# A linear-attention and sparse-FFN kernel: the q products come first in each step, q copies are issued one slot earlier, sums and loads are reordered

## The chip, the cores and the metric

The kernel runs on one core of one Trainium2 chip. A core has a matrix engine (TensorE, PE in the profile, its weight loads PEld), a vector engine (VectorE, DVE), a scalar engine (ScalarE, ACT), GpSimd (POOL) and SyncE (SP), which here issues nearly all DMAs. Each engine works through its own list of instructions in order. The metric is device time in microseconds; lower is better.

## The reference

The input x has two batches of 1024 rows of 512. The reference computes, with a layernorm before and after each of two blocks and a residual around each:

```python
x = x + _layernorm(_L0_attn_ref(_layernorm(x, axis=-1), Wq, Wk, Wv, Wo), axis=-1)
x = x + _layernorm(_L0_ffn_ref(_layernorm(x, axis=-1), w_gate, w_up, w_down), axis=-1)
```

The attention is linear and causal: 16 query heads, 4 key and value heads, head size 128. q and k are rotated (rope), then passed through elu(.) + 1; a scan keeps a running sum of k v^T and of k, and each output is q times the state, divided by q times the sum of k. The feed-forward block is `silu(x Wg) * (x Wu)`, of which the two largest of every four neighbours (by absolute value) are kept, times `w_down`; the hidden width is 2048.

## The kernel before

**Strassen-like products.** Every large product is cut into 2 x 2 blocks and done with seven block products instead of eight (`strassen`, L114). Its generator yields after each of the seven, so that the caller can put other work between: the products come in the order 1, 2, 6, 5, 7, 4, 3. Products 1, 6, 7 and 4 add up in one PSUM bank ("cb"), product 2 has "ca", products 5 and 3 add up in "ce". After 1, 6 and 7 ScalarE copies the bank's partial sum (`keep`, L125), and DVE adds it to another bank (L134, L144, L150). The weight combinations that the products need are sums of weight quarters (`sums`, L419). For the first pass over q, k, v they are made on the chip from loaded quarters; for everything later POOL prepares them in the background (`prepare`, L453) and SP stores them to DRAM and loads them again.

**Steps.** The attention goes through 16 steps: two passes (each has half of the heads) over eight chunks of 128 rows of both batches. For step n + 1, `kv_products` (L652) and `q_products` (L675) make k, v and four blocks of q. `features` (L622) does the rope and elu of a block: two DVE multiplies (L629, L635), a POOL add (L641), two ScalarE functions (L643, L644), a DVE combine (L645). A q block is then turned in 32 x 32 squares by DVE (L549), stored to DRAM (`q_store`), loaded in another order (`q_load`, four DMA issues, L562) and copied by ScalarE into place (`q_copy`, L712), which finishes the transpose.

Each step has four slots, one for each group (batch, key head). `scores(n, i)` (L715) multiplies the transposed k with the copied q and DVE masks the result; `attend(n, i)` (L731) multiplies by v and by the state; DVE takes the reciprocal of the denominator and ScalarE scales four heads (L754). The output block goes the same way over DRAM (`o_store`, `o_load`, `o_copy`), and the output projection of step n - 1, `o_products` (L809), runs in step n. In the second pass its end is a layernorm and residual: POOL adds the first pass's part (L843), DVE normalizes, POOL adds x (L846), and SP stores the rows for the feed-forward part.

**Order.** PE, POOL and SP keep the order in which the program text emits instructions (`manual_schedule`, L877). On DVE and ACT a planner orders by its own estimate, except for the very first part on DVE. In a step, the calls `first(i)` and `second(i)` (L908, L929) hold the slot's copies, stores, loads, attend and scores; the products of the next step and of the previous output lie between them. Before the change the order of a step is: kv products of n + 1 in slot 0, q products in slots 0 to 2, output products in slots 2 and 3. The four sums of `o_copy(n, 3)` (L799 to L803) are emitted together; one of them (L802) runs on POOL. `q_copy(n, i + 1)` is issued in `first(i)`, right before `attend(n, i)` and `scores(n, i + 1)` of the same slot.

**Ends.** At the start x, the weight quarters, the rope table, the next x blocks and the output weights are loaded on two queues (L434 to L444). At the end of the attention the first feed-forward rows are normalized and transposed (`ffn_input`, L193), and the first two gate products are run early (L1022 on). The feed-forward part goes over four groups of 512 rows: gate and up products, the choice of two of four, the down product, and `ffn_output` (L354), which normalizes and adds the residual for four row tiles.

Of the kernel before, what the change touches and what calls it, by code (L numbers as in the profile page):

```python
# [35 lines left out]
def kernel(  # L36
# [21 lines left out]

    ident = const.tile([P, P], F32, name="ident")
# [13 lines left out]
    eps = const.tile([P, 1], F32, name="eps")  # L73
    nc.gpsimd.memset(eps, LN_EPS)
# [24 lines left out]
    def layernorm_scale(src, tag):  # L99

        st = small.tile([P, nc.vector.BN_STATS_DIM], F32, tag=f"st{tag}", name="st")
        nc.vector.bn_stats(st, src)
        mv = small.tile([P, nc.vector.BN_AGGR_DIM], F32, tag=f"mv{tag}", name="mv")
        nc.vector.bn_aggr(mv, st)
        sd = small.tile([P, 1], F32, tag=f"sd{tag}", name="sd")
        nc.scalar.activation(sd, mv[:, 1:2], AF.Sqrt, bias=eps)
        rs = small.tile([P, 1], F32, tag=f"rs{tag}", name="rs")
        nc.vector.reciprocal(rs, sd)
        return mv[:, 0:1], rs
# [4 lines left out]
    def strassen(pools, shape, product, c11, c12, c22, done):  # L114
# [24 lines left out]
        e = bank("ce")  # L139
# [4 lines left out]
        nc.vector.tensor_tensor(c22, s3, e, ALU.add)  # L144
# [5 lines left out]
        nc.vector.tensor_tensor(c12, s2, e, ALU.add)  # L150
# [170 lines left out]
    def down(hf):  # L321


        def product(bank, i, start):
# [3 lines left out]
            for jb in range(NJB):  # L328
                for j in range(2):
                    for k in range(2):  # L330
                        nc.tensor.matmul(
                            bank[:, j, :],
                            hf[jb][hi][:, k, j * P : (j + 1) * P],
                            w[:, jb, k, :],
                            start=(start and jb == 0 and j == 0 and k == 0),
                            stop=(jb == NJB - 1 and j == 1 and k == 1),
                            skip_group_check=True,
                        )
# [10 lines left out]
                lambda t: nc.scalar.copy(y[:, 0:2, 256:512], t),  # L349
            )  # L350
# [3 lines left out]
    def ffn_output(m, tt, xt_, y):  # L354
        b, c = place(m, tt)
        mean, rs = layernorm_scale(y, "y")
        yn = pool["ln"].tile([P, DM], F32, tag="ln", name="fyn")
        normalize(yn, y, mean, rs)
        nc.gpsimd.tensor_tensor(yn, xt_, yn, ALU.add)  # L359
# [59 lines left out]
    def sums(t, engine):  # L419
        a11, a12, a22, s2, s4, s3, s1 = (t[:, i] for i in range(7))  # L420
        for o, i0, i1, op in (
            (s1, s3, a22, ALU.add),
            (s3, a11, s3, ALU.subtract),
            (s2, s1, a11, ALU.subtract),
# [9 lines left out]
    xt = {0: load_x(0)}  # L434
# [3 lines left out]
    load_quarters(wq_sb, q_quarter, (nc.scalar, nc.sync))  # L438
    rope_sb = rawp.tile([P, NC, 3, HD // 2], F32, name="rope_sb", bufs=1)
    nc.scalar.dma_start(out=rope_sb, in_=rope.rearrange("(c p) t d -> p c t d", p=P))  # L440
    xt[1] = load_x(1)
    wo_sb = new_factors("wo", 4, 256)
    load_quarters(wo_sb, o_quarter, (nc.sync,))
    xt[2] = load_x(2)  # L444
# [177 lines left out]
    def features(src, c, dst):  # L622

        half = HD // 2
        cos = rope_sb[:, c, 0, :].unsqueeze(1).broadcast_to([P, 8, half])
        sin = rope_sb[:, c, 1:3, :].unsqueeze(1).broadcast_to([P, 4, 2, half])
# [25 lines left out]
    def kv_products(n):  # L652
        c = n % NC
# [13 lines left out]
        features(raw, c, f)  # L667
# [7 lines left out]
    def q_products(n):  # L675
        c = n % NC
        raw = [rawp.tile([P, REP, HD], F32, tag="raw", name="qraw", bufs=4) for _ in range(3)]

        def feature(i, src):
            f = qp.tile([P, REP, HD], F32, tag="qf", name="qf", bufs=1)  # L680
            features(src, c, f)
# [28 lines left out]
    def q_copy(n, i):  # L710
        t = qp.tile([P, REP, P], F32, tag="qT", name="qT")
# [64 lines left out]
    later = []  # L776
# [13 lines left out]
    def o_copy(n, i, t=None):  # L790
# [6 lines left out]
        else:  # L797
            t1, t2, t3, t4 = (factor(n, 3 + k, 1) for k in range(4))
            nc.vector.tensor_tensor(by_block(t1), t, by_block(of[n, 0]), ALU.subtract)  # L799
            nc.vector.tensor_tensor(t2, of[n, 2], t1, ALU.subtract)  # L800
            t3_engine = nc.gpsimd if n + 1 < STEPS else nc.vector
# [47 lines left out]
    def load_pass(place, name, blocks, width, of_):  # L849
        t = new_factors(name, blocks, width)  # L850
        for f in range(7):
            nc.sync.dma_start(out=t[:, f], in_=of_[:, f])
# [258 lines left out]
```

## Time and profile before

The times are of whole runs; the profile is one of these executions.

| what | value |
|---|---|
| median of 5 runs | 1494.82 us (1491.52 to 1501.59) |
| the profiled execution, its time | 1501.59 us |
| its span (first to last instruction) | 1499.9 us |
| mean granted TensorE clock | 0.955 |
| PE busy | 1335.4 us, 89% |
| DVE busy | 866.8 us, 58% |
| ACT busy | 518.6 us, 35% |
| POOL busy | 324.6 us, 22% |
| first score of step 0, 1, 8, 15 | 60.9, 95.7, 469.8, 822.4 us |
| first gate product, end of the early gates and last output product | 876.3, 917.9 us |

A line of the profile's lists gives an engine, a line of the kernel (L12) and what it made from what, then the idle time of the engine before it and what ended that wait. In the list of waits the numbers are microseconds in total, how often, and the longest. In the timeline they are the start, the duration, and in brackets the idle time before. The table by stage has for each stretch its length, the busy time of each engine with its instructions, the granted clock, the DMA share and GB/s.

### The profile page before, as it was taken

The page shows a single profiled execution, that of the slowest core. Times are in us where ns is not written, and L with a number is a line of the kernel's source. Part 1 is how long each engine was busy: PE and PEld are TensorE (multiplying, and loading weights), DVE is VectorE, ACT ScalarE, POOL GpSimd, SP SyncE. Part 2 cuts the span into 40 slices and gives each one's busy share as a digit, 9 for nine tenths or more (in the row PEclk, how much of TensorE's full clock was granted, in tenths as well). Part 3 has the DMA queues.
Part 4 walks back from the last instruction along what each step waited for, and adds up shares of the span by engine and source line. Part 5 has one row for each costly group of instructions (what it writes and reads, how often), then busy time and mean ns, then how long its engine had stood idle before and what let it go on. Part 6 is the DMA issues. An engine that isn't in the chain of part 4 may idle for free. (4 is left out here: it accounts for less than half of the span.)

```text
span 1499.9 us, 17626 instructions
## 1 busy us (share of the span) xinstructions
PE 1335.4 (89%) x5888; PEld 1047.6 (70%) x5888; DVE 866.8 (58%) x1550; ACT 518.6 (35%) x1053; POOL 324.6 (22%) x259
## 2 busy tenths in 40 slices
PE   4779888897888879899889599999999999999997
PEld 2446566565566547666666488888888888888886
DVE  5657656745645546675666523982667166725662
ACT  2444444433333334444434332321332133213311
POOL 0323223222323414434442111011001100110001
PEclk9979989999998889999999799999999999999999
DMA  6344566565876657765655635545654465445412
GB/s 227 108 161 142 183 200 203 176 196 172 269 238 175 183 203 245 246 215 180 226 186 174 218 99 195 157 124 175 197 150 124 175 198 151 123 176 173 116 57 84
DMA packets 199019, 262.56 MB, mean 175 GB/s; under 512 B 18192, under 2 KB 124688, under 8 KB 194832
## 3 DMA queue, kind: packets, MB, share of 16 engines
q1 hardware_dynamic: 196800, 259.07, 54.3%
q10 hardware_dynamic: 2128, 2.36, 0.5%
q8 instruction: 47, 0.77, 0.2%
q14 instruction: 44, 0.36, 0.1%
HBM read 177.73 MB, written 83.62 MB: 174 GB/s over the span
## 5 line engine op out<-in xcount | busy, mean ns | idle before, releaser
L125 ACT COPY u<-cb 128x512 f32<-128x512 f32 (+1 forms) x252 | 126.4, 501 | 468.3 <-PE cb L225 178.6
L641 POOL TENSOR_TENSOR u<-u,r 128x512 f32<-128x512 f32 x80 | 106.3, 1330 | 359.8 <-DVE r L635 183.3
L817 PE MATMUL cb<-wo,of 128*128 128x256 f32 x512 | 142.9, 429 | 36.6 <-ACT u L125 31.7
L817 PEld LDWEIGHTS cb<-wo,of 128*128 128x128 f32 x512 | 108.3, 217 | 73.4 <-issue 45.1
L718 PE MATMUL sc<-qT,kT 128*128 128x512 f32 x128 | 78.1, 696 | 71.6 <-ACT qT L712 71.6
L608 PE MATMUL cb<-wq,xf 128*128 128x512 f32 x256 | 124.0, 607 | 1.7 <-ACT u L125 1.7
L225 PE MATMUL cb<-fxt,wgu 128*128 128x256 f32 x512 | 117.9, 381 | 1.4 <-ACT u L125 1.4
L225 PE MATMUL cb<-fxnT,wgu 128*128 128x256 f32 x512 | 116.9, 379 | 0.0
L645 DVE SCALAR_TENSOR_TENSOR qf<-u,r 128x512 f32<-128x512 f32 x64 | 67.0, 1047 | 81.0 <-ACT r L644 69.3
L754 ACT ACTIVATE o<-nm,den 128x128 f32<-128x128 f32 x256 | 75.7, 365 | 108.6 <-DVE den L751 102.9
L225 PEld LDWEIGHTS cb<-fxt,wgu 128*128 128x128 f32 x512 | 96.6, 190 | 17.0 <-ACT u L125 4.2
L745 PE MATMUL nm<-v,am 128*128 128x129 f32 x512 | 100.6, 288 | 7.7 <-ACT state L767 5.0
L225 PEld LDWEIGHTS cb<-fxnT,wgu 128*128 128x128 f32 x512 | 97.0, 190 | 13.2 <-ACT u L125 0.2
L643 ACT ACTIVATE r<-u 128x512 f32<-128x512 f32 x80 | 50.5, 631 | 133.2 <-POOL u L641 132.6
L173 POOL TENSOR_TENSOR h<-h 128x512 f32<-128x512 f32 x16 | 23.9, 1496 | 332.3 <-DVE ht L170 332.3
L608 PEld LDWEIGHTS cb<-wq,xf 128*128 128x128 f32 x256 | 49.2, 195 | 61.1 <-issue 49.4
L744 PE MATMUL nm<-state,qT 128*128 128x129 f32 x448 | 90.1, 284 | 1.1 <-DVE state L769 1.1
L745 PEld LDWEIGHTS nm<-v,am 128*128 128x128 f32 x512 | 81.7, 205 | 10.2 <-ACT state L767 5.4
L144 DVE TENSOR_TENSOR y<-u,ce 128x256 f32<-128x256 f32 (+1 forms) x20 | 9.5, 474 | 126.2 <-ACT u L125 126.2
L744 PEld LDWEIGHTS nm<-state,qT 128*128 128x128 f32 x448 | 75.1, 201 | 9.9 <-issue 6.2
L718 PEld LDWEIGHTS sc<-qT,kT 128*128 128x128 f32 x128 | 21.2, 209 | 77.3 <-ACT qT L712 77.3
L608 PE MATMUL cb<-wkv,xf 128*128 128x256 f32 x256 | 71.0, 402 | 4.3 <-ACT u L125 2.9
(150 smaller groups left out, 2577.2 us busy)
## 6 DMA issues: line engine op xcount, KB each, us to landing
wgu<-gs SPq DMA_DIRECT2D x112, 256.0 KB, 2.8
wgu<-us SPq DMA_DIRECT2D x112, 256.0 KB, 2.7
wd<-d_dram SPq DMA_DIRECT2D x28, 1024.0 KB, 4.8
qb<-blocks SPq DMA_DIRECT2D x64, 256.0 KB, 2.1
landed<-qb SPq DMA_DIRECT2D x256, 64.0 KB, 2.2
ob<-blocks SPq DMA_DIRECT2D x60, 256.0 KB, 2.3
landed<-ob SPq DMA_DIRECT2D x240, 64.0 KB, 2.2
xf<-xf SPq DMA_DIRECT2D x16, 896.0 KB, 4.7
```

The lines of the kernel that those rows point to most:

```text
L125: nc.scalar.copy(t, b)
L173: (engine or nc.gpsimd).tensor_tensor(b12, b22, b12, ALU.subtract)
L225: nc.tensor.matmul(bank[:, j, :], w[:, k, j, :], xf[xi][:, k, :], start=(start and j == 0 and k == 0), stop=(j == 1 and k == 1), skip_grou ...
L608: nc.tensor.matmul(bank.rearrange("p h d -> p (h d)"), x_[:, xi, k, :], w[:, wi, k, :], start=(start and k == 0), stop=(k == 1), skip_grou ...
L641: nc.gpsimd.tensor_tensor(u, u, r, ALU.add)
L643: nc.scalar.activation(r, u, AF.Relu, scale=-1.0)
L645: nc.vector.scalar_tensor_tensor(dst, u, 0.0, r, ALU.max, ALU.add)
L718: nc.tensor.matmul(sc.rearrange("p h t -> p (h t)"), kT[n][:, 2 * b + j, :], qT[n, i].rearrange("p h t -> p (h t)"), start=True, stop=True,)
L744: nc.tensor.matmul(dst, q[:, h, :], state[b, j], start=True, stop=False)
L745: nc.tensor.matmul(dst, a[:, h, :], v, start=(c == 0), stop=True)
L754: nc.scalar.activation(t[:, h, :], nmv[:, h // 2, h % 2, 0:HD], AF.Copy, scale=den[:, h // 2, h % 2 : h % 2 + 1],)
L817: nc.tensor.matmul(bank.rearrange("p h d -> p (h d)"), of[n, xi][:, k, :], w[:, wi, k, :], start=(start and k == 0), stop=(k == 3), skip_g ...
```

## The change

In each step the q products of step n + 1 now come first (slots 0 and 1), then the kv products (slots 1 and 2), then the output products of step n - 1 (slots 2 and 3). `q_copy` is issued one slot earlier, with three buffers in place of two, and the stores and loads before it move to match. Three of the four output sums move into `o_sums`, which is called after the kv features. The residual add and the store behind it move into later slots. In each half slot the output's store, the q load and the output's load come in this order. The weight loads of the second pass come in the order in which the products use them, a few per slot. The rope table is loaded a chunk at a time.

At the start, x is loaded in two halves on two queues, the weight sums run on POOL instead of DVE, later x blocks and output weights are loaded behind the first step's input, the square root's table is loaded by a small activation ahead of its first use, and the q products of step 1 run in full ahead of step 0, its kv products inside step 0. At the attention's end the feed-forward transposes begin one step earlier, in another PSUM pool, and the first gate runs between the slots. The ring of feed-forward weights has 15 buffers, not 16. In the last down product, products 5 and 3 finish one row tile before the other; the last two row tiles take their statistics in two halves and add the residual on DVE.

```diff
     def layernorm_scale(src, tag, st=None):
+        if st is None:
+            st = layernorm_stats(src, tag)[:, 0:1, :]
+        else:
+            nc.vector.bn_stats(st[:, 1, :], src)
...
-        e = bank("ce")
+        rows = range(shape[1]) if split else [slice(0, shape[1])]
+        es = [bank("ce")[:, r] for r in rows]
+        e = es if split else es[0]
...
-        nc.vector.tensor_tensor(c12, s2, e, ALU.add)
+        for r, er in zip(rows, es):
+            nc.vector.tensor_tensor(c12[:, r], s2[:, r], er, ALU.add)
...
+            split = isinstance(bank, list)
+            blocks = [(jb, j) for jb in range(NJB) for j in range(2)]
+            if split:
+                blocks.sort(key=lambda block: block[1])
...
-        nc.gpsimd.tensor_tensor(yn, xt_, yn, ALU.add)
+        (nc.vector if last else nc.gpsimd).tensor_tensor(yn, xt_, yn, ALU.add)
...
-    xt = {0: load_x(0)}
+    def load_rope(n):
+        t = rawp.tile([P, 3, HD // 2], F32, tag="rope", name="rope")
+        c = n % NC
+        nc.sync.dma_start(out=t, in_=rope[c * P : (c + 1) * P])
+        rope_sb[n] = t
+
+    xt, rope_sb = {}, {}
+    xt[0] = xp.tile([P, B, DM], F32, tag="x", name="x")
+    for b, engine in enumerate((nc.sync, nc.scalar)):
+        engine.dma_start(out=xt[0][:, b, :], in_=x[b, 0:P, :])
...
-    load_quarters(wq_sb, q_quarter, (nc.scalar, nc.sync))
-    rope_sb = rawp.tile([P, NC, 3, HD // 2], F32, name="rope_sb", bufs=1)
-    nc.scalar.dma_start(out=rope_sb, in_=rope.rearrange("(c p) t d -> p c t d", p=P))
-    xt[1] = load_x(1)
+    load_quarters(wq_sb, q_quarter, (nc.sync, nc.scalar))
+    load_rope(0)
+    root = const.tile([P, 1], F32, name="root")
+    nc.scalar.activation(root, eps, AF.Sqrt)
...
-        t = qp.tile([P, REP, P], F32, tag="qT", name="qT")
+        t = qp.tile([P, REP, P], F32, tag="qT", name="qT", bufs=3)
...
+    def o_sums(n):
+        t2, t3, t4 = (factor(n, 4 + k, 1) for k in range(3))
+        nc.vector.tensor_tensor(t2, of[n, 2], of[n, 3], ALU.subtract)
+        t3_engine = nc.gpsimd if n + 1 < STEPS else nc.vector
+        t3_engine.tensor_tensor(t3, t2, of[n, 0], ALU.subtract)
+        nc.vector.tensor_tensor(t4, of[n, 1], t2, ALU.subtract)
...
+        for i in (1, 2, 6, 5, 7, 4, 3):
+            f = FACTORS[i][0]
+            nc.sync.dma_start(out=t[:, f], in_=of_[:, f])
+            yield
...
-            finish(sums(wkv_sb, nc.vector))
+            finish(sums(wkv_sb, nc.gpsimd))
             step_input(0, xns)
-            finish(sums(wq_sb, nc.vector))
+        xt[1] = load_x(1)
+        load_rope(1)
+        load_quarters(wo_sb, o_quarter, (nc.sync,))
+        xt[2] = load_x(2)
+        wq_sums = sums(wq_sb, nc.gpsimd)
+        run(wq_sums, 2)
         finish(kv_products(0))
+        finish(wq_sums)
...
             def first(i):
...
-                if i < 3:
-                    q_copy(n, i + 1)
+                if i < 2:
+                    q_copy(n, i + 2)
                 elif more:
-                    q_copy(n + 1, 0)
+                    q_copy(n + 1, i - 2)
...
+                if i < 2 and n > 0:
+                    o_copy(n - 1, i + 2)
+                elif i > 1 and more:
+                    o_copy(n, i - 2)
                 if i == 2 and more:
                     q_store(n + 1, 3)
+                if i > 0 and more:
                     o_store(n, i - 1)
                 elif i == 0 and n > 0:
                     o_store(n - 1, 3)
+                if i == 0:
+                    q_load(n, 3)
+                elif more:
+                    q_load(n + 1, i - 1)
+                if i > 0 and more:
+                    o_load(n, i - 1)
+                elif i == 0 and n > 0:
+                    o_load(n - 1, 3)
+                if i == 2 and n + 2 < STEPS:
+                    load_rope(n + 2)
+                next(preparing, None)
+
+            def second(i):
+                for k in ((0,), (1, 2), (), ())[i] if more else ():
+                    q_store(n + 1, k)
                 attend(n, i)
...
             first(0)
+            if n > 0:
+                run(qpr, 2)
...
+            second(0)
+            first(1)
+            finish(qpr)
...
+            kvp = kv_products(n + 1)
+            run(kvp, 3)
...
             second(1)
             first(2)
+            finish(kvp)
...
+            if n > 0:
+                o_sums(n - 1)
...
+            run(opr, 2)
...
             second(2)
             first(3)
...
+            run(opr, 1)
+            k_transposed(n + 1)
+            run(opr, 2)
...
             second(3)
             finish(opr)
```

## The prediction

> **What bounds the kernel now.** First the page's head and its row of slices for TensorE and its clock.
>
> ```profile
> span 1499.9 us, 17626 instructions
> PE 1335.4 (89%) x5888; PEld 1047.6 (70%) x5888; DVE 866.8 (58%) x1550; ACT 518.6 (35%) x1053; POOL 324.6 (22%) x259
> PE   4779888897888879899889599999999999999997
> PEclk9979989999998889999999799999999999999999
> ```
>
> TensorE is the fullest engine, but it has holes in the first 25 of 40 slices and its clock dips there. Next comes the table by stage. I cut it at the first score matmul of steps 1, 8 and 15, and at the first gate product after the attention.
>
> ```profile
> 0.00:95.71 95.71, 57.78 (x193) 34.63 (x193) 62.39 (x118) 37.51 (x80) 24.34 (x26) 0.92 0.45 157
> 95.71:469.81 374.10, 323.36 (x1389) 234.34 (x1389) 218.75 (x405) 150.06 (x340) 107.09 (x85) 0.92 0.61 195
> 469.81:822.41 352.60, 311.78 (x1341) 223.07 (x1341) 212.92 (x390) 148.41 (x335) 126.06 (x100) 0.95 0.64 205
> 822.41:917.86 95.45, 76.83 (x347) 63.00 (x346) 35.38 (x87) 30.70 (x68) 12.75 (x10) 0.87 0.46 146
> 917.86:1499.90 582.04, 565.64 (x2625) 492.52 (x2623) 337.33 (x552) 151.90 (x231) 54.34 (x39) 1.00 0.49 151
> ```
>
> After each stretch's length stand PE, PEld, DVE, ACT and POOL busy, then the granted clock. The last stretch, the feed-forward part, runs TensorE at 97% and full clock: little is to be had there but its tail. The other 918 us are the place. Third, TensorE's waits.
>
> ```profile
> PE sc L718 <- ACT qT L712: 71.6, 25, 8.3
> PE cb L817 <- ACT u L125: 31.7, 13, 4.6
> PE pst L539 <- DVE x L112: 16.9, 2, 8.7
> ```
>
> The scores wait for the q copy (71.6 us), the output products for ScalarE's copy of a partial product (31.7), the first transposes for the first normalize (16.9). Last, a window at one long score wait, with the plainer kind from step 12 below it.
>
> ```profile
> 184.80 1.77 POOL L802 TENSOR_TENSOR of<-of 128x512 f32<-128x512 f32 x1 [8.35 <-DVE of L800]
> 186.53 2.48 POOL L641 TENSOR_TENSOR u<-u,r 128x512 f32<-128x512 f32 x2
> 187.82 0.63 ACT L643 ACTIVATE r<-u 128x512 f32<-128x512 f32 x1 [6.16 <-POOL u L641]
> 190.62 0.60 ACT L712 COPY qT<-landed 128x512 f32<-128x512 f32 x1
> 191.27 2.07 PE L718 MATMUL sc<-qT,kT 128*128 128x512 f32 x2 [8.22 <-ACT qT L712]
> ...
> 726.17 1.14 ACT L754 ACTIVATE o<-nm,den 128x128 f32<-128x128 f32 x4 [2.13 <-DVE den L751]
> 727.19 0.63 ACT L712 COPY qT<-landed 128x512 f32<-128x512 f32 x1
> ```
>
> At 184.80 POOL stood 8.35 us at an output sum; the feature adds came behind it, ScalarE stood at the feature, and the q copy, which needs neither, stood behind that. At 727 the copy merely stands behind the attend's own scalings, and the scores wait 2.23 us after attend has ended.
>
> **The floor of a step.** Step 14 runs from 777.75 to 822.41, 44.66 us, and its rows show waits of 1.66 and 0.19: 42.8 without them. Steps 1 to 7 also transpose two x blocks, 0.43 each (the kf transposes take 709.63 to 710.06): 43.7.
>
> **Steps 1 to 7 (374.1 us, floor 306).** Of 68 us over the floor, waits of the kinds above are 36.8 + 15.7 + 1.5 = 54. That leaves 14 for half clock and small bubbles.
> - Copies a slot ahead, three qT buffers. A q copy now has some 11 us between its issue and its scores instead of following the same attend. The scaling that holds it is 1.14 us, the long chain above about 6; both fit. I take all 36.8.
> - Sums behind the features. POOL's L802 no longer stands ahead of L641, so the 8 us chain goes. The sums' readers (products 6, 5, 4 of the output) move later too.
> - Output products. Product 7 waits for the copy after product 6. In between lay one product, 1.73 us; now the four kf transposes lie there too (+0.43), and the scaling of attend 2 (done about 2 us after it) is past. Of 15.7 I take 12.
> - The price: q products 7, 4, 3 now follow one another, and 3 waits for a sum that follows 7: copy 0.58 + add 0.69 + hand-overs of 0.05 to 0.1 = 1.4 us, against product 4's 1.72. In kv, 0.37 + 0.42 + 0.15 = 0.95 against 0.86. Idle engines would cost 0.1 a step; with DVE busy 218.75 of 374 I take 1.5. From below it is 0 (its cover is there when DVE is free), from above 4 (both chains behind two DVE operations of 0.69 each).
> - SP queue. Every block store, block load and preparing transfer still goes out; the order changes, so that the output's load now stands close behind its own store, with the q load (four issues, 1.75) between. The store's landing is 2.3, so SP stands about 0.6 a slot; four slots, 2.4 of 47 us, and what is late is a copy with a slot to spare. The rope block is one more issue of 0.4 a step. The residual adds and the x2 store move one slot on, past the features on POOL; the x2 rows are read eight steps later. Cost nothing; without the cover each POOL add is 1.27.
> - Weight loads spread over slots, in the order of use: step 7 to 8 and the 59.1 us of step 9 (520.90 to 579.98) hold bursts of block loads behind them. I count this in the waits already.
>
> New step: 43.7 + 3.9 (1.5 for the new chains, 0.5 left of the output waits, 1.9 of half clock and DMA) = 47.6; seven are 333, **-41**. Bounds: 44.7 a step (-61) and 52 (-10).
>
> [...] The rows: clock 0.92 over 374 us, and 14 us left when floor and waits are taken off. [...]
>
> **Steps 8 to 14 (352.6, floor 300).** Over the floor 53; waits 25.8 + 15.1 + 2.0 = 43. The same edits, no x blocks: 42.8 + 3.1 = 45.9 a step, 321.6, **-31**. Bounds 43.8 (-46) and 49.5 (-6).
>
> **Start (95.71).** Now: x normalized at 17.25 for the second batch, because DVE stands 6.97 us at the next x block; xf ready at 24.6, kv done at 30, q at 44.6, first score 60.9. After: the x1 load stands behind the xf store on SP, so its stats cannot come first. From x landed (4.67): stats 0.69, aggregate 0.18, square root 0.29 (its table load of 1.28 is earlier), reciprocal 0.16, normalize 0.55; second batch +1.3; transposes 1.09, copies and subtracts 2.4: xf at about 11. The wkv sums on POOL cost 4 x 1.27 = 5.1 instead of 2.8 on DVE, from the last quarter (issued 1.80, 7.1 to land) to 14; the products meet them as they come. The wq sums are twice as wide, 2.5 each (an estimate from 1.27): q starts at 16, ends at 29. That is 15 us earlier. Then DVE sets the pace: 62.4 busy now, less 7.6 of sums, 55 us from 4 on; at 80% busy step 1 starts at 72: **-24**. Bounds: DVE full (62, -33), and feature chains that give most back (-12).
>
> [...] The row: x of 512 KB was issued at 0.80 and read at 4.67; the 256 KB wkv quarters issued beside it took 4.1 to 7.1. [...]
>
> **Last step and gates (95.45).** PE busy 76.8 at clock 0.87. Waits: 8.2 at scores, 4.0 at an output product behind a DVE aggregate, 2.7 + 1.4 at transposes. Gate 0 now lies between the slots, the FFN transposes begin a step earlier, in another PSUM pool. The waits (18.6 idle) shrink to 7 and half of the clock loss (0.13 x 95 = 12) goes: **-17**. Bounds -26, -4.
>
> **Tail.** From TensorE's end (1490.63) to the last POOL add's end (1496.89) are 6.2 us for two row tiles. After: half-width add 0.42, half stats 0.4, aggregate 0.18, root 0.29, reciprocal 0.16, normalize 0.55, add on DVE 0.69, hand-overs 0.5: 3.2, **-3**; the other tile's chain lies under the last 3.4 us of matmuls. The ring of 15 buffers costs nothing while TensorE shows no wait for its loads; a lost cover is 1.7 us, one product, per load.
>
> Sum: -41 -31 -24 -17 -3 = **-116**. The profiled execution took 1501.59 (span 1499.9), 6.8 above the median; its share of the change is put on the median: 1494.8 - 116 = **1379**.
>
> **Rivals.**
> - *The new chains take half back* (0.28). The three q products, the kv tail and the DVE backlog of four q features in 1.5 slots cost 4 us a step over 14 steps, 56 in all: 1435. For it: DVE is the second fullest engine. Against: ScalarE and DVE have 40% free.
> - *Gone in full* (0.12): steps at 44.7 and 43.8, -61 -46 -24 -17 -3 = -151, 1344.
> - *Slower* (0.06): SP. Store, its landing 2.3, load 1.75 and 2.2 to land are now one chain inside each half slot. If ScalarE reaches a copy before it has landed, the partial-product copies stand behind it and TensorE stops. At 3 us a slot, 60 slots are 180: 1494.8 - 116 + 180 = 1559. It decides from 116 / 60 = 1.9 us a slot. Against: no wait of ScalarE on a landing stands in the list now.
> - *No change* (0.02): every score wait turns into one at the q or kv sums: 1495.
>
> **How the numbers follow.** The likeliest has 0.52. A change under 0.5% can't be told from none. Faster 0.92, same 0.02, slower 0.06. The range leaves out the slower and equal cases and a little of each end: 1340 to 1440.
>
> **What would show it.** Score waits under 10 us in total; steps of 46 to 48; clock above 0.95 in steps 1 to 14; step 1's first score near 72; the sum L802 behind L641 on POOL. Wrong if "ce" products of q or kv wait for DVE over 2 us a step, or ScalarE waits for landings.

## The result and the profile after

The change gains nothing: 1499.38 us median with it and 1496.48 without it, ratio 1.0014 (95% interval 1.0005 to 1.0024), which is 0.14% slower. The forecast was 1379 us. The profiled execution took 1501.02 us; its page begins so, with the rows of slices for TensorE and its clock:

```profile
span 1499.3 us, 17668 instructions
PE 1337.8 (89%) x5888; PEld 1038.7 (69%) x5888; DVE 853.4 (57%) x1548; ACT 529.5 (35%) x1062; POOL 328.6 (22%) x265
PE   5688898898878797897888899999999999999997
PEclk9898999999999999999999999999999999999999
```

The table by stage, cut as before at the first score of steps 1, 8 and 15 and at the end of the early gates (length, then PE, PEld, DVE, ACT, POOL busy, granted clock, DMA share, GB/s):

```profile
0.00:94.07 94.07, 59.95 (x192) 35.87 (x193) 57.36 (x97) 41.48 (x78) 39.05 (x33) 0.88 0.45 149
94.07:475.84 381.77, 328.69 (x1397) 232.99 (x1397) 211.94 (x414) 155.81 (x348) 101.88 (x85) 0.93 0.61 198
475.84:848.83 372.99, 317.49 (x1346) 221.82 (x1345) 214.52 (x408) 151.72 (x345) 122.59 (x101) 0.95 0.63 202
848.83:919.50 70.67, 66.38 (x334) 55.18 (x333) 30.13 (x71) 28.16 (x61) 10.70 (x8) 1.00 0.42 145
919.50:1499.30 579.80, 565.29 (x2625) 492.83 (x2623) 339.43 (x558) 152.31 (x231) 54.40 (x39) 1.00 0.49 152
```

The start became 1.6 us shorter (forecast: 24 shorter), steps 1 to 7 7.7 longer (forecast: 41 shorter), steps 8 to 14 20.4 longer (forecast: 31 shorter), the last step with the gates 24.8 shorter (forecast: 17), the rest 2.2 shorter (forecast: 3). One cut misleads: the first feed-forward transposes, with a wait of 3.8 us at them, moved from step 15 into step 14. Step 14 went from 44.7 to 53.3 us. With the cut at step 14, steps 8 to 13 became 11.8 longer (307.9 to 319.7) and steps 14 and 15 with the gates 16.1 shorter together (140.1 to 124.0). That is close to the 17 of the forecast.

TensorE's waits, with total, number and longest:

```profile
PE cb L637 <- ACT u L133: 68.3, 44, 4.9
PE pst L568 <- DVE kf L674: 20.9, 7, 5.1
PE pst L568 <- DVE x L119: 9.9, 2, 8.4
PE sc L745 <- ACT qT L739: 9.1, 1, 9.1
PE ce L637 <- DVE v L155: 8.5, 9, 2.3
PE cb L637 <- DMA xf<-xf: 8.3, 3, 6.7
PE cb L849 <- ACT u L133: 5.3, 10, 1.1
PE cb L637 <- DMA wq<-wq_dram: 5.2, 1, 5.2
```

What was to go, went: the scores' waits from 71.6 to 9.1 us and the output products' from 31.7 to 5.3. New ones took their place: 68.3 at the q and kv products behind ScalarE's copy of a partial product, 20.9 at the transposes of the k features (none before), 13.5 at loads. The first of these stood in the list of before as

```profile
PE cb L608 <- ACT u L125: 4.6, 9, 1.3
```

All of TensorE's idle time (gaps over 30 ns) was 155.2 us before and is 154.0. Its busy time rose by 2.4 us. Of it 102.2 us lay at half clock before and 94.5 after; half of that is lost (in before's trace the attend's pairs of matmuls follow one another every 0.22 us at full clock, from 830.03 on, and every 0.43 us at half, from 844.30 on), so this part fell by 3.9. The rest of the busy time rose by 6.3, which no row here explains.

Sorted by the product just ahead, the 68.3 us are: product 4 directly behind product 7, 26.4 in kv (16 times) and 20.7 in q (15 times); product 6 of kv behind product 2, 13.5 (10 times); the rest small. A window of TensorE in one step (start, duration, idle time before in brackets):

```profile
270.02 1.88 PE L637 MATMUL cb<-wq,xf 128*128 128x512 f32 x4
272.58 1.98 PE L637 MATMUL cb<-wq,xf 128*128 128x512 f32 x4 [0.68 <-ACT u L133]
274.40 1.88 PE L637 MATMUL ce<-wq,xf 128*128 128x512 f32 x4
276.12 1.03 PE L637 MATMUL cb<-wkv,xf 128*128 128x256 f32 x4
276.98 1.03 PE L637 MATMUL ca<-wkv,xf 128*128 128x256 f32 x4
281.16 1.13 PE L637 MATMUL cb<-wkv,xf 128*128 128x256 f32 x4 [3.16 <-ACT u L133]
...
285.86 1.03 PE L637 MATMUL cb<-wkv,xf 128*128 128x256 f32 x4
288.21 1.13 PE L637 MATMUL cb<-wkv,xf 128*128 128x256 f32 x4 [1.32 <-ACT u L133]
290.04 2.07 PE L637 MATMUL ce<-wkv,xf 128*128 128x256 f32 x4 [0.70 <-DVE v L155]
```

At 272.58 and 288.21 product 4 follows product 7 in the same bank and waits for the copy in between. At 281.16 it is product 6 of kv, which waits for the copy after product 1 and has only product 2 (0.86 us from start to start) for cover. Before, the attend and the next scores lay between 7 and 4, since the cut into slots fell there (after five of the seven products); now it falls after four (q) and after three (kv). ScalarE around that second wait:

```profile
277.25 0.63 ACT L672 ACTIVATE r<-u 128x512 f32<-128x512 f32 x1 [1.69 <-POOL u L670]
277.79 0.60 ACT L739 COPY qT<-landed 128x512 f32<-128x512 f32 x1
278.41 1.28 ACT L673 ACT_TABLE_LOAD   x1
279.70 0.63 ACT L673 ACTIVATE r<-r 128x512 f32<-128x512 f32 x1
280.24 0.61 ACT L672 ACTIVATE r<-u 128x512 f32<-128x512 f32 x1
280.76 0.35 ACT L133 COPY u<-cb 128x256 f32<-128x256 f32 x1
```

The copy of 0.35 us could start from 277 on and stands behind two q features, a q copy and a table load. The k features' waits have another chain. POOL at step 11:

```profile
670.83 1.68 POOL L500 TENSOR_TENSOR wraw<-wraw 128x512 f32<-128x512 f32 x1
672.59 1.59 POOL L501 TENSOR_TENSOR wraw<-wraw 128x512 f32<-128x512 f32 x1
674.15 1.71 POOL L670 TENSOR_TENSOR u<-u,r 128x512 f32<-128x512 f32 x1
```

Two sums of the background preparation stand ahead of the k feature's add. TensorE waited for that feature until 678.41, 4.52 us.

### The profile page after: what moved, and what is told of

It reads as the page before. It is cut to its first block, busy times and chain, and to the rows that moved or that the text cites. A ratio compares the mean times of both kernels' runs of the same rounds, so it can differ in the third digit from the quotient of the medians.

```text
span 1499.3 us, 17668 instructions
## 1 busy us (share of the span) xinstructions
PE 1337.8 (89%) x5888; PEld 1038.7 (69%) x5888; DVE 853.4 (57%) x1548; ACT 529.5 (35%) x1062; POOL 328.6 (22%) x265
## 3 DMA queue, kind: packets, MB, share of 16 engines
q1 hardware_dynamic: 198976, 260.38, 54.5%
## 4 chain that ended last, share of the span: by engine, by line
PE 63%; DVE 13%; ACT 7%; DMA 6%; POOL 4%; issue 4%; SPq 3%; ACTq 0%; DVEq 0%; POOLq 0%
PE cb L237 14%; PE ce L237 7%; PE cb L849 7%; PE cb L346 6%; PE cb L637 5%; PE ce L346 3%; PE ca L237 3%; PE ce L849 3%; POOL u L670 3%; PE ce L637 2%; PE nm L772 2%; PE sc L745 2%; PE nm L771 2%; DVE blocks L578 2%; SPq L591 2%
## 5 line engine op out<-in xcount | busy, mean ns | idle before, releaser
L637 PE MATMUL cb<-wq,xf 128*128 128x512 f32 x256 | 133.9, 648 | 41.8 <-ACT u L133 28.4
L849 PE MATMUL cb<-wo,of 128*128 128x256 f32 x512 | 129.3, 398 | 5.4 <-ACT u L133 5.3
L637 PEld LDWEIGHTS cb<-wq,xf 128*128 128x128 f32 x256 | 49.7, 202 | 109.2 <-issue 58.6
L849 PEld LDWEIGHTS cb<-wo,of 128*128 128x128 f32 x512 | 101.5, 202 | 31.1 <-ACT u L133 10.6
L237 PEld LDWEIGHTS cb<-fxnT,wgu 128*128 128x128 f32 x512 | 97.1, 190 | 13.5 <-issue 0.5
L772 PE MATMUL nm<-v,am 128*128 128x129 f32 x512 | 97.4, 280 | 3.6 <-ACT state L794 3.6
L637 PEld LDWEIGHTS cb<-wkv,xf 128*128 128x128 f32 x256 | 49.2, 201 | 62.8 <-ACT u L133 50.4
L674 DVE SCALAR_TENSOR_TENSOR qf<-u,r 128x512 f32<-128x512 f32 x64 | 53.0, 829 | 60.7 <-ACT r L673 57.2
L772 PEld LDWEIGHTS nm<-v,am 128*128 128x128 f32 x512 | 78.5, 197 | 5.1 <-ACT state L794 4.0
L745 PE MATMUL sc<-qT,kT 128*128 128x512 f32 x128 | 67.2, 607 | 9.1 <-ACT qT L739 9.1
```

Source lines behind the costliest of these rows:

```text
L237: nc.tensor.matmul(bank[:, j, :], w[:, k, j, :], xf[xi][:, k, :], start=(start and j == 0 and k == 0), stop=(j == 1 and k == 1), skip_grou ...
L637: nc.tensor.matmul(bank.rearrange("p h d -> p (h d)"), x_[:, xi, k, :], w[:, wi, k, :], start=(start and k == 0), stop=(k == 1), skip_grou ...
L674: nc.vector.scalar_tensor_tensor(dst, u, 0.0, r, ALU.max, ALU.add)
L745: nc.tensor.matmul(sc.rearrange("p h t -> p (h t)"), kT[n][:, 2 * b + j, :], qT[n, i].rearrange("p h t -> p (h t)"), start=True, stop=True,)
L772: nc.tensor.matmul(dst, a[:, h, :], v, start=(c == 0), stop=True)
L849: nc.tensor.matmul(bank.rearrange("p h d -> p (h d)"), of[n, xi][:, k, :], w[:, wi, k, :], start=(start and k == 0), stop=(k == 3), skip_g ...
```

## The experiments

Two theories stood against each other. One: each new wait has its own cause (the cut between products 7 and 4, the place of the preparation on POOL and on the load queue), and undoing that cause returns its time. The other: the step is bound by something else (ScalarE's queue, the load queue), and a wait that is taken away comes up elsewhere. Each ratio is to the kernel before, with its 95% interval; after stands at 1.0014.

One thing bears on nearly all of these runs. On ScalarE and DVE the planner orders the work anew for every kernel, so an edit moves more than its own lines. Of ScalarE's 1062 instructions 133 are out of after's order in `five_two`, 113 in `q_five_two`, 127 in `prep_first`; 92 are out of `prep_first`'s order in `prep_xf`. Each ratio is thus the worth of an edit together with the order that the planner gave it. Only the third landed buffer leaves the order alone but for one instruction on ScalarE and six on DVE (`landed_three` against after, `five_two_landed` against `five_two`, `all_four` against `five_two_prep_xf`).

**The cut of the chains.** `five_two` cuts both chains after five products again and keeps everything else of after.

```diff
             if n > 0:
-                run(qpr, 2)
+                run(qpr, 3)
             run(wo_loads, 2)
             second(0)
...
             kvp = kv_products(n + 1)
-            run(kvp, 3)
+            run(kvp, 5)
```

> The changed kernel, with the cut between products moved: five q products before attend 0 and two after, five kv products before attend 1 and two after. Theory A (the bank chain): product 4 adds into the bank that ScalarE has just begun to copy after product 7, so it needs other work between; 20.7 us of q waits and 26.4 us of kv waits at that place, with 8.5 at product 3 of kv behind them, fall under 10 together: 1435 to 1455. Theory B (DVE and the feature chains set the step, a wait taken away comes back at the next place): 1488 to 1502.

Measured: 1481.61 us, 0.989 (0.9846 to 0.9934), between the two theories' ranges.

`q_five_two` and `kv_five_two` do one of the two edits.

> The changed kernel with the cut of the q products alone moved to five and two. Theory A: the 20.7 us at product 4 of q go, some clock with them: 1475 to 1484. Theory B: 1492 to 1502.

Measured: 1493.82 us, 0.9968 (0.9945 to 0.999), in theory B's range. The wait at product 4 of q did go (20.7 to 1.3 us), but in the kv chain product 6 rose from 13.5 to 24.0 and product 4 from 26.4 to 32.7.

> The changed kernel with the cut of the kv products alone moved to five and two. Theory A: the 26.4 us at product 4 and the 8.5 at product 3 of kv go, and k is ready earlier, so some of the 17.2 us at its transposes too: 1455 to 1472. Theory B: 1490 to 1502.

Measured: 1486.39 us, 0.992 (0.9888 to 0.9951), again between the ranges; the k features' waits rose from 20.9 to 38.6 us. The parts are worth about 0.5% and 0.9% from after, both together 1.2%. The cut, with what the planner made of it, has a price of its own, some 18 us. TensorE's waits of `five_two` show what is left:

```profile
PE cb L637 <- ACT u L133: 55.0, 29, 6.1
PE pst L568 <- DVE kf L674: 28.9, 8, 6.4
```

Product 4 directly behind 7 fell from 47.1 us to 1.2; product 6 of kv now waits 24.7 in all (13.5 in after), product 4 of kv 10.5 where it stands behind the scores, and the k features came later (20.9 to 28.9). Some 46 us of waits were removed and the idle time fell by 13.3 (154.0 to 140.7): much of what was taken away came up at other products and transposes.

**The output sums alone.** `before_sums` is the kernel before with three of the four sums of `o_copy(n, 3)` in `o_sums`, issued later in the step as in after.

```diff
+            if n > 0:
+                o_sums(n - 1)
             run(opr, 2)
```

> The kernel before, with one part of the change alone: the three output sums are issued behind the q features, ahead of the output products. The prediction's reading: the long score waits (8.2, 8.3 and 7.6 us) go, and the half clock behind them: 1460 to 1478. The rival: ScalarE's copy stands behind something else as long: 1490 to 1500.

Measured: 1490.87 us, 0.996 (0.9937 to 0.9982), in the rival's range. TensorE's waits:

```profile
PE sc L718 <- ACT qT L712: 72.6, 29, 7.5
...
PE cb L821 <- ACT u L125: 13.4, 7, 4.3
PE cb L821 <- POOL of L806: 13.4, 6, 3.1
```

The output products' waits for the copy fell from 31.7 to 13.4 us, but 13.4 us returned as a wait for the moved sum on POOL. The scores' waits did not shrink in total; those over 5 us went from four with 30.1 us to four with 24.2. So POOL's stand at the sum, which the forecast read as the head of the long score waits, is not what holds most of the q copies. With it gone they still came late. In after, with the copies a slot ahead, they do not.

**The place of the preparation.** In `prep_first` the background preparation is issued at the head of the slot again, as before the change.

```diff
             def first(i):
+                next(preparing, None)
...
-                next(preparing, None)
```

> The changed kernel with one call moved back: the background weight preparation is advanced at the head of each half slot, as before the change, instead of at its tail, behind the block loads. Theory C (POOL): in the changed kernel the preparation's stores leave SP late, POOL stands 182 us ahead of its sums until they land (39 before), and the feature adds queue there; with the call at the head this falls under 60, the 17.2 us at the k transposes and part of the copy waits go: 1470 to 1487. Theory B (the waits come back at the next place): 1494 to 1503.

Measured: 1478.96 us, 0.9882 (0.9856 to 0.9908), in theory C's range. TensorE's and then the load queue's waits:

```profile
PE cb L637 <- ACT u L133: 69.7, 45, 5.0
PE cb L637 <- DMA xf<-xf: 17.5, 4, 9.4
...
PE pst L568 <- DVE kf L674: 4.1, 2, 3.7
```

```profile
SPq L591 <- ACT qT L739: 143.4, 37, 10.1
```

The k features' waits are gone (20.9 to 4.1), so the preparation's place had most to do with them, though POOL's idle time ahead of its sums fell only from 182.1 to 124.4 us, not under 60. In exchange xf lands later, since the queue now stands 143.4 us at block loads that wait for a buffer which ScalarE has yet to copy out (82.6 in after). Of the 22.6 us between the two spans, 9.1 are idle time and 13.7 are busy time of TensorE; 94.5 us of it were at half clock in after, 69.6 are here.

The other way round, `before_prep_last` moves the preparation behind the loads in the kernel before.

```diff
             def first(i):
-                next(preparing, None)
...
                 if i < 2 and n > 0:
                     o_load(n - 1, i + 2)
+                next(preparing, None)
```

> The kernel before, with this one part of the change alone: the preparation is advanced at the tail of each half slot. Theory C: POOL's waits before the preparation's sums rise from 39 to over 100 us and the features' scores wait longer: 1505 to 1530. If the place of the call costs nothing by itself: 1490 to 1500.

Measured: 1500.15 us, 1.0022 (1.0005 to 1.0039). POOL's idle time ahead of the sums rose from 39.2 to 66.0 us, not over 100; the scores' waits rose from 71.6 to 96.7 and the output products' fell from 31.7 to 12.2. In time it costs almost nothing there, where k is made at the head of the step and transposed in the third slot.

`five_two_prep` has both edits, the cut and the place.

> Both: the cut at five and two for q and kv, and the preparation at the head. Theories A and C together: the 25 us at the k transposes left in the first go as well, 1447 to 1466. Theory B: 1477 to 1486, as with the cut alone.

Measured: 1488.01 us, 0.9921 (0.9892 to 0.995), above both ranges. Two edits worth 18 and 20 us from after are worth 11 together by the medians (14 by the ratio): the second theory has its part. Against `five_two` the place of the preparation makes no difference that is clear of the intervals. The waits at xf loads are 24.0 us here, product 6 of kv has 27.0.

**The table loads.** In these traces ScalarE loads a table, 1.28 us each time, whenever it changes between the square root of a layernorm and the exponential of a feature (22 loads before, 28 after) or the silu of the feed-forward part (14 and 16); with the first one the change raised these loads from 37 to 45. `no_root` leaves the square root out of the attention's layernorms (the scale is 1/variance, so the numbers differ).

```diff
+        if tag in ("a", "o"):
+            nc.vector.reciprocal(rs, mv[:, 1:2])
+            return mv[:, 0:1], rs
         nc.scalar.activation(rs, mv[:, 1:2], AF.Sqrt, bias=eps)
```

> The changed kernel without the square root in the attention's layernorms (the scale is one over the variance, so the numbers differ), and so without ScalarE's changes of table between root and exponential: 45 table loads, 57.7 us of ScalarE, fall under 20. Theory A with C (ScalarE's copies are late because of what stands ahead of them): the first score's wait of 9.1 and the 4.9 in the first q products mostly go, 1480 to 1492. If the tables are beside the path: 1495 to 1503.

Measured: 1477.34 us, 0.9865 (0.9842 to 0.9889), with 17 table loads; this is below both ranges. The first score came at 47.4 us (58.6 in after), step 1 at 83.3 (94.1), and product 6 of kv waited 5.1 us in place of 13.5. By stage the start became 10.8 us shorter and steps 1 to 7 18.9 shorter, steps 8 to 13 4.0 longer and the last two with the gates 3.7 longer.

`before_no_root` is the same edit in the kernel before (again the scale is 1/variance).

> The kernel before without the square root in the attention's layernorms (the scale is 1/variance, so the numbers differ), as no_root is for after. If the new order made the cost of the table changes, before gains little by it, under 8 us: 1488 to 1496 us, the start and steps 1 to 7 within 5 us of their 95.7 and 374.1 us. If the table changes cost the same in both orders, it gains as after did, 18 to 26 us: 1470 to 1479 us.

Measured: 1501.68 us, 1.0024 (0.9999 to 1.0049): nothing gained. The start became 3.9 us shorter and steps 1 to 7 3.5 shorter, steps 8 to 13 10.4 longer. The table loads went from 37 to 14 and the idle time from 155.2 to 159.3. So leaving out the roots is worth nothing in the old order and some 22 us in the new one, where the q features and the partial sums' copies meet the roots on ScalarE. How much of the 22 is the loads themselves and how much the planner's new order was not separated (50 of ScalarE's remaining 1002 instructions are out of after's order).

**The xf load.** `prep_xf` is `prep_first` with the reload of xf two slots earlier.

```diff
             first(0)
+            if NC <= n + 2 < STEPS:
+                step_input_again(n + 2)
...
-            elif n + 2 < STEPS:
-                step_input_again(n + 2)
```

> The kernel after with the preparation issued first in a slot again (as in the run prep_first, 1479.0 us) and with the reload of xf (steps 8 to 15) issued at the head of a step, two slots earlier than after has it. Theory: prep_first made three or four xf loads land late (17.5 us of waits of TensorE where after has 8.3), because the queue that carries them waits behind the copies of ScalarE; two slots earlier they land in time, and the 17.5 us go: 1461 to 1468 us. Rival: the queue is late by the same amount wherever a load stands in it, so that what moves up pushes the q and o blocks back and the score and output waits rise again: 1476 to 1484 us.

Measured: 1490.18 us, 0.9944 (0.9914 to 0.9974): slower than `prep_first`, which neither side expected. The xf waits did go, but the k features' waits came back (15.9 us, 4.1 in `prep_first`), and there are two waits for wq, 9.5 us in all. Idle time rose only 3.6 us; busy time rose 12.1, with 96.9 us at half clock in place of 69.6. Part of that is the execution that was profiled: at 1493.94 us it is one of the two slowest of seven, which go from 1482.79 to 1494.2 us, and, as an estimate from their spans and granted clocks (0.97 to 0.956), from 89 to 131 us at half clock.

`five_two_prep_xf` adds the cut.

> As prep_xf, with product 7 and product 4 of the q and kv chains parted again (five products and two, as in the run five_two). five_two and prep_first gained 15 and 18 us alone and only 8 us together (1488.0 us). Theory: together they failed to add because xf came late (24.0 us of waits); with the earlier reload these go and the time is 1461 to 1468 us, about that of prep_xf or below. Rival: the two fixes compete for ScalarE and for the queue behind its copies, not for the xf load; the waits move on to the kf transposes and the products behind the features and the time stays at 1480 to 1490 us.

Measured: 1490.84 us, 0.9937 (0.9916 to 0.9958). The xf waits are gone and the time did not move from `five_two_prep`, as the rival said; the load itself was not what kept the fixes from adding up.

**The landed blocks.** The q and o blocks that come back from DRAM share two buffers. `all_four` gives them a third on top of `five_two_prep_xf`.

```diff
-        t = qp.tile([P, 4, REP, 32], F32, tag="landed", name="landed")
+        t = qp.tile([P, 4, REP, 32], F32, tag="landed", name="landed", bufs=3)
...
-        for name, bufs in (("ring", 15), ...
+        for name, bufs in (("ring", 14), ...
```

> As five_two_prep_xf, with three buffers in place of two for the landed q and o blocks (the feed-forward's ring of weights gives one of its 15 buffers for it). Theory that the load queue is held by ScalarE's copies of the landed blocks (143 to 150 us of the queue's waits in prep_first and five_two_prep, 83 us in after): with a third buffer that wait falls under 80 us and the time is 4 to 10 us below five_two_prep_xf. Rival: the queue's waits cost nothing once xf is early, and the time equals five_two_prep_xf's within 3 us; the feed-forward's stage loses nothing by the buffer in either case.

Measured: 1468.19 us, 0.9789 (0.9766 to 0.9812). 22.6 us below `five_two_prep_xf`, more than either side gave. The queue's wait for ScalarE's copies of q blocks fell from 156.2 to 97.0 us, not under the 80 expected, and the feed-forward stage stayed (580.2 and 580.0 us).

Then each edit alone on this ground. `landed_three` is after with the third buffer and nothing else.

> The kernel after with three buffers in place of two for the landed q and o blocks, nothing else (one ring buffer of the feed-forward less, as in all_four). Theory A, the load queue held by the landed blocks is what turned the old waits into new ones: 1474 to 1482 us, with the kf and xf waits (17.2 and 8.3 us) gone. Theory B, the new waits have causes of their own (product 4 behind product 7, the preparation's place on the loading queue and on POOL), and the buffer pays only when these are gone: 1488 to 1499 us, with 40 us and more of product 4's waits still there.

Measured: 1488.17 us, 0.9935 (0.9893 to 0.9977). Product 4 behind 7 still waits 49.3 us, the k features 21.9. Theory B holds as to the waits: the buffer alone doesn't remove them. Even so it is worth 0.8% from after, with the order on TensorE, ScalarE, DVE and POOL as good as unchanged.

`prep_xf_landed` is `all_four` with after's cuts.

> all_four with product 4 directly behind product 7 again in the q and kv chains (the cuts 4 and 3 of after). If the adjacency has a price of its own, the waits of product 4 are there again (30 to 50 us in place of 10 to 18) and the time is 10 to 20 us above all_four: 1478 to 1488 us. If the adjacency only filled time in which TensorE would have waited elsewhere, the time is all_four's within 4 us: 1464 to 1472 us.

Measured: 1476.5 us, 0.9854 (0.9832 to 0.9877). Product 4 behind 7 waits 45.5 us again and the time is 8.3 above `all_four`: the cut costs, though less than the waits it shows, and the time lies between the two ranges.

`five_two_landed` is after with the old cuts and the third buffer, the preparation and xf where after has them.

> all_four with the preparation behind the loads of the slot and the xf reload in the third slot again, as after has them: the parted chains and the third buffer alone. If POOL's and the queue's order of the preparation still costs, the kf waits stay at 20 us and more and the time is 1475 to 1483 us. If the third buffer makes that order free, 1466 to 1472 us.

Measured: 1468.34 us, 0.9796 (0.9774 to 0.9819), the time of `all_four`, though the k features still wait over 20 us, which was expected only together with 1475 to 1483 us. TensorE's and the load queue's waits:

```profile
PE cb L637 <- ACT u L133: 55.2, 28, 5.3
PE pst L568 <- DVE kf L674: 22.6, 7, 4.5
PE sc L745 <- ACT qT L739: 9.4, 1, 9.4
```

```profile
SPq L591 <- ACT qT L739: 34.8, 15, 7.8
```

Here are the four corners:

| | two landed buffers | three |
|---|---|---|
| cut after 4 (q) and 3 (kv) | 1.0014 | 0.9935 |
| cut after 5 and 5 | 0.989 | 0.9796 |

Within the intervals the two edits add: 0.8% and 1.2% one by one, 2.2% together. Against after the span is 32.5 us shorter: 17.2 of idle time and 15.6 of busy time, of which half clock (94.5 to 72.8) explains 10.9. The place of the preparation doesn't add: it gains 20 us on after, nothing clear of the intervals on `five_two` (`five_two_prep`), and with the third buffer it (with the xf load) gives nothing.

**The end of the attention alone.** `before_ends_sums` is `before_sums` with after's last step and first gates.

```diff
                 xts, loaded, xns = begin_ffn()
+                parts = ffn_input(xns, ps_mm, "mm", nc.vector)
...
+        run(parts, 3)
+        xf = next(parts)
+        early = [gate(xf, jb, gates[jb], ps_mm, loaded[jb].get) for jb in range(2)]
         first(0)
         second(0)
+        run(early[0], 4)
```

> The kernel before with two parts of the change alone: the output factors' sums issued behind the loads of the slot (as in before_sums, 1490.9 us), and after's arrangement of the last step and of the first gates. Theory: these two parts carry their gain without the rest, and the last step is as short as in after (70.7 us where before has 95.5): 1491 - 25 = 1466, 1462 to 1470 us, which beats both kernels. Rival: the last step is short in after only because its q chain comes first and its blocks are a slot ahead; then the stage keeps 85 us or more and the time is 1478 us or above.

Measured: 1487.74 us, 0.9916 (0.9888 to 0.9944). Steps 14 and 15 with the gates take 136.7 us (141.2 in `before_sums`, 124.0 in after). A score wait of 7.2 us in step 15 and a half-clock stretch of 10.2 us stay. This is the rival's side: the arrangement of the last step and the gates brings 4.5 us by itself, and the other 12 of that stage in after need the rest of the change; the score wait that stays names the q copies' place.

## Why the prediction was wrong, step by step

- *Copies a slot ahead, "I take all 36.8"* and *output products, "I take 12"*: the waits named went (71.6 to 9.1, 31.7 to 5.3). Right as waits, wrong as time.
- *The price: "q products 7, 4, 3 now follow one another ... I take 1.5".* This is the step that failed most. It priced product 3, which waits for DVE's sum, and overlooked product 4: it adds into the same bank that ScalarE copies out after product 7. Product 3 waited 8.5 us for DVE in the whole run, 0.6 a step. Product 4 waited 47.1 in 31 chains, and with product 6 of kv (13.5) the chains wait 69 us in all, 4.9 a step. In time the old cut brings back 18 us, since other waits come up behind these. The rival "the new chains take half back" had 4 a step and the wrong engine; its 1435 us still lacked the rest.
- *The sums "behind the features ... so the 8 us chain goes".* It goes, but the preparation was moved too, and its sums (1.6 us each) stood ahead of the k features' adds. POOL waited 39.2 us ahead of preparation sums before and 182.1 after, and TensorE waited 20.9 us for the k features that come behind them. The forecast named the preparing transfers only on the load queue, at no cost. `prep_first` takes that wait to 4.1 us.
- *"SP queue ... Cost nothing".* A third landed buffer, which lets that queue run on and changes next to nothing else, gave 11.2 us on after and 13.3 on `five_two`. The cover claimed, a copy with a slot to spare, was there for the scores; what stood behind the blocks on the queue, xf and wq, had none (13.5 us). The rival "Slower" looked at the same queue but at the wrong customer: ScalarE waited on landed q blocks for only 3.2 us in all.
- *The start, "DVE sets the pace ... -24".* Measured -1.6. The first score came at 58.6; with the 35 us of step 0, the forecast's 72 for step 1 needed it at 37. ScalarE, not DVE, held it, in the window ahead of that score:

```profile
50.47 1.28 ACT L114 ACT_TABLE_LOAD   x1
51.77 0.29 ACT L114 ACTIVATE rs<-mv,eps 128x1 f32<-128x1 f32 x1
52.08 1.28 ACT L673 ACT_TABLE_LOAD   x1
53.37 0.63 ACT L673 ACTIVATE r<-r 128x512 f32<-128x512 f32 x1
53.91 0.61 ACT L672 ACTIVATE r<-u 128x512 f32<-128x512 f32 x1
54.54 1.28 ACT L114 ACT_TABLE_LOAD   x1
55.83 0.29 ACT L114 ACTIVATE rs<-mv,eps 128x1 f32<-128x1 f32 x1
56.15 1.28 ACT L673 ACT_TABLE_LOAD   x1
57.44 0.63 ACT L673 ACTIVATE r<-r 128x512 f32<-128x512 f32 x1
57.98 1.12 ACT L739 COPY qT<-landed 128x512 f32<-128x512 f32 x2
```

  Roots of one layernorm alternate with exponentials of q features: four table loads, 5.1 us, with the score's copy behind them. Without the roots the start is 10.8 us shorter (`no_root`), so about half of the missing 22 us goes with these roots and their loads. The other half stays open. In the working no table load but the first was counted.
- *Last step and gates, -17*: -16.1 with the cut at step 14. Right in size; but by `before_ends_sums` the arrangement alone brings only 4.5 of it. *Tail, -3*: -2.2 for the whole feed-forward stage.
- *Half clock.* The prediction put down the 14 us left over in steps 1 to 7 to half clock and small bubbles, and let 1.9 a step stay. The term was too small: TensorE worked 47.7 us of these steps at half clock, of which half, 23.9, is lost (the floor of 306 was too high: without that loss the seven steps' busy time is 299.5). After, it is 46.9 us, so this loss stayed as it was. In the whole run the busy time at half clock fell by 7.7 us, a gain of 3.9. All the half clock within the span, 135.4 us before and 117.2 after, would make 9 us by the same share. Part of that time TensorE stood idle; the count of the time in which it worked gives 3.9.

Of the signs that the prediction named, the score waits came out (9.1 us); the steps (54.5 and 53.3 us on average, not 46 to 48), the clock (0.93 and 0.95) and step 1's first score (94) did not. Neither of its two signs of being wrong appeared: product 3 waited 0.6 us a step for DVE, and ScalarE 3.2 us in all for q blocks.

What stays open: why the preparation's place helps after and not `five_two`, and why `prep_xf` is slower than `prep_first`. Both were measured; the half clock and the planner's order differ with them, and neither was held still. Open too are the 89 us between the best run (1468.2) and the forecast. In `five_two_landed` steps 1 to 7 take 359.1 us (forecast 333), and steps 8 to 13 take 310.3, no less than the 307.9 before. TensorE's waits for ScalarE's copies at q and kv products are the largest there still (26.1 us in steps 8 to 14).

## What to carry to other kernels

When a chain of products moves, list for each product what it waits for in its new place, bank by bank, and what lies in between; work that looked like an interruption was the cover of a copy. A wait that is removed is worth its time only when the next one behind it is found and priced too: here 89 us of waits at scores and output products went and about as much came back, until the cut and the buffer were changed together. Count queue positions for the background work as for the main work, on each engine that it uses.

## What the runs showed of the hardware

A wait of TensorE had a second price in these runs, half clock behind it: by the table below it followed none of 293 waits of 0.3 to 1 us, 7 of 171 of 1 to 2 us and 202 of 253 above 2 us. Over the 18 profiles of this family of kernels, past the first 100 us, I took each wait that had no other above 1 us in the 10 us before and 6 us after it, and looked for half clock from its start to 8 us past its end:

| wait | waits | followed by half clock | mean half-clock time where it followed |
|---|---|---|---|
| 0.3 to 1 us | 293 | 0 | |
| 1 to 2 us | 171 | 7 | 3.9 us |
| 2 to 2.5 us | 67 | 37 | 3.5 us |
| 2.5 to 3.5 us | 80 | 62 | 4.2 us |
| 3.5 to 5 us | 53 | 50 | 5.1 us |
| over 5 us | 53 | 53 | 7.5 us |

The half-clock stretches recorded in the steps of before and after are 3.4 us long or a multiple of it (6.8, 10.2, 13.7, 20.5). As an estimate from the table, ten waits of 1 us cost 10 us, and two of 5 us cost the same and 5 to 7 more. So kernels with nearly the same idle time can differ: `prep_first` and `prep_xf` have 144.9 and 148.5 us of it and are 15.5 us of span apart. The waits' lengths do not settle it alone: past the first 100 us after and `prep_first` have 20 and 18 waits over 2 us, 7 over 3.5 each, and 95.4 and 78.8 us at half clock (to the end of the clock's record). Nor is it the same in each execution of one kernel: by the spans and granted clocks of after's 54 runs (0.956 to 0.97) they have 89 to 132 us at half clock, at 1491.97 to 1506.92 us (an estimate: in the traces of before and after the granted clock is either full or half), and each us of it goes with about a third of a us of time.

A change of ScalarE's table cost 1.28 us in all 45 loads of after, and next to nothing beside it: in the window above the root begins 0.02 us after its table load ends, at 51.75, and the load at 52.08 begins 0.02 us after that root.
